# Moving GpSimd's sums for M and the dot products of layer 1 within a planned four-layer graph kernel

## Chip, cores and metric

The kernel runs on one core of a Trainium2 chip. The metric is the device time of one execution in microseconds. Before the change the median of three runs is 2234.3 us (2232.62 to 2236.04).

## What is computed

The input is 128 graphs of 128 nodes with 512 features, in float32, and one adjacency matrix of 128 by 128. Four layers follow one another, each a residual with a layer norm. Cut to what matters:

```python
y  = einsum('nm,bmd->bnd', adj, x);  x = norm(x + y @ W + bias)                # layer 0
q, k, v = x @ Wq.T, x @ Wk.T, x @ Wv.T                                         # layer 1
rel = adj.T * (q @ k.T);  rel = rel / norm_of_rows(rel);  x = norm(x + rel @ v)
h = x @ W2;  e = leaky(h @ a1 + (h @ a2).T) * adj                              # layer 2
x = norm(x + elu(softmax(e) @ h + beta * h))
x = norm(x + max(relu(A[:, :, None] + (C - A)[..., None])))                    # layer 3, A = adj x
```

In layer 1 the product of Wq and Wk is formed once, as M, so that q k' becomes (x M) x'. In layer 2 the scores h a1 and h a2 become dot products of the rows of x with two vectors W2 a1 and W2 a2 ("the dots"). They are taken of x before its layer norm and put right afterwards with the mean and the reciprocal deviation.

## The kernel before

The graphs are taken in 32 groups of four. Every group goes through the four layers, and the groups overlap like the stages of a pipeline: a group starts 28 slots after the one before it, and in one stretch of 28 slots (about 67 us) TensorE works on layer 0 of one group, layer 1 of the same and of the next, and layers 2 and 3 of older ones.

The order of the work is written by hand. `TABLE` gives each piece of a group's work a place in slots; `times(g)` adds 28 slots per group; `emit` collects (place, function) pairs; at the end the pieces are sorted by place and called (line 783). Each engine then runs its instructions in that order, since the engine wrappers keep the program's order. So the places decide only what comes before what on each of the engines; the waits between engines decide when.

The four large products (by W for y, by M, by Wv for v, by W2 for z) use a scheme with seven block products where a plain one needs eight. `left_factors` makes the four sums or differences of blocks on GpSimd (tile `s_x` for the products by M and Wv, `s_y`, `s_z` for the others); `product` issues seven steps on TensorE in the order 1, 2, 6, 5, 7, 3, 4. Steps 1, 2 and 4 read blocks of the transposed input itself (`xT`), steps 6 and 3 need the second and the fourth of GpSimd's sums, step 5 the first and step 7 the third. A finished region of PSUM is taken to SBUF by a copy on ScalarE or an addition on VectorE. Steps 1, 6, 7 and 4 share one PSUM region, so step 4 cannot start until VectorE's addition of step 7 (`tT<-r_m,tT`) has read it.

The pieces around the change, with the names that the profile shows:

- `x_sums` (left_factors, line 594): four GpSimd additions of 128x512 elements, `s_x<-xT`, `s_x<-s_x,xT`, `s_x<-xT`, `s_x<-xT,s_x`.
- `bias` (line 428): four GpSimd additions `x<-x,bias_sb` for the next group, each after TensorE's `p_y` of that graph has read x. After them come the four sums `s_y`.
- `residual` (line 545): VectorE, `x<-p_o,rn,x`, then `st` and `mv` (statistics).
- `dots` (line 559): VectorE, two `scr<-x,wa` per graph, eight per group, both operands in SBUF, each with an accumulator.
- `norm1` (line 379): VectorE's `ve`, then GpSimd's power `rstd`.
- `scale` (line 574): VectorE's `d<-mv,wa_sum,d` twice and `d<-d,rstd`. Layer 2's `p_s` on TensorE reads `d`.
- `elu` (line 716): VectorE's `x<-c,x` and `x<-m,x`, of an older group, again with both operands in SBUF.

Of the kernel before, what the change touches and what calls it, by code (L numbers as in the profile page):

```python
# [29 lines left out]
def kernel(  # L30
# [196 lines left out]
    def row(at, step, n=G):  # L227
        return [at + i * step for i in range(n)]


    TABLE = dict(
        load=[-20], y=row(0.5, 1), bias=row(1.3, 1), y_sums=row(5.2, 0.5), y_w=row(7, 1, 7),
        stats0=row(14.4, 0.4), norm0=[16.2], apply0=row(16.8, 0.33),
        turn=row(21.4, 1), turn_blocks=row(18.4, 0.6),
        move=row(20.5, 0.1), x_sums=row(25.3, 0.5), m=row(28, 1, 7), scores=row(36.5, 1),
        masked=[39.95], squares=[40.4], turn_rel=[40.3],
        move_rel=row(41.2, 0.1), inverse=[42.5], v=row(42, 1, 7), attend=row(50.6, 1),
        residual=row(51.0, 1), dots=row(54.2, 1.1), norm1=[55.2], scale=[58.8],
        apply1=row(65.4, 0.33),
        spread=[61.6], leaky=[62.0], weighted=[63.4], greatest=[64.3], exps=[64.4],  # L240
        divide=[65.8], turn_att=[68.6], with_beta=[69.0], gather=row(71.5, 1),
# [15 lines left out]
            scale=[5.6], apply1=row(24.3, 0.8), spread=[6.9], leaky=[7.4], weighted=[9.0],  # L257
# [8 lines left out]
            m=[0.0, 1.73, 3.46, 5.2, 7.4, 9.1, 10.8], scores=row(12.7, 0.9), masked=[16.4],  # L266
            squares=[17.2], turn_rel=[17.1], move_rel=row(18.0, 0.1), inverse=[20.0], v=[16.7, 18.4, 21.0, 22.7, 25.3, 27.9, 30.5],
            attend=row(33.2, 0.86), residual=row(34.1, 1.65), norm1=[40.65], dots=row(40.7, 1.53),
            scale=[47.0], apply1=row(47.5, 0.8), spread=[48.9], leaky=[49.4], weighted=[51.0],
# [544 lines left out]
```

## Time and profile before

The profile is one execution of 2234.4 us.

| engine | busy us | share | instructions |
|---|---|---|---|
| TensorE matmul (PE) | 2182.9 | 98% | 11073 |
| TensorE weight load (PEld) | 1842.1 | 82% | 11073 |
| VectorE (DVE) | 1794.9 | 80% | 3534 |
| ScalarE (ACT) | 980.0 | 44% | 1936 |
| GpSimd (POOL) | 983.1 | 44% | 743 |

A line of the timeline gives the start and the duration in us, the engine, the operation and the tiles as out<-in; a bracket gives the idle time of the engine before it and what ended it. A line of the costliest groups gives the count, the busy time, the mean duration of one and the idle time before. All calculations share one helper line (L26), so instructions are told apart by their tiles.

The work of a group repeats almost to 10 ns, so times below are often given relative to T, the start of the fourth `p_o` of a group (of its last graph's attention product). For the groups counted from 0, T is 299.45 for group 3, 366.27 for group 4 and 1042.01 for group 14.

### The profile page before, as it was taken

The page shows a single profiled execution, that of the slowest core. Times are in us where ns is not written, and L with a number is a line of the kernel's source. Part 1 is how long each engine was busy: PE and PEld are TensorE (multiplying, and loading weights), DVE is VectorE, ACT ScalarE, POOL GpSimd, SP SyncE. Part 2 cuts the span into 40 slices and gives each one's busy share as a digit, 9 for nine tenths or more (in the row PEclk, how much of TensorE's full clock was granted, in tenths as well). Part 3 has the DMA queues.
Part 4 walks back from the last instruction along what each step waited for, and adds up shares of the span by engine and source line. Part 5 has one row for each costly group of instructions (what it writes and reads, how often), then busy time and mean ns, then how long its engine had stood idle before and what let it go on. Part 6 is the DMA issues. An engine that isn't in the chain of part 4 may idle for free.

```text
span 2234.4 us, 31661 instructions
## 1 busy us (share of the span) xinstructions
PE 2182.9 (98%) x11073; PEld 1842.1 (82%) x11073; DVE 1794.9 (80%) x3534; ACT 980.0 (44%) x1936; POOL 983.1 (44%) x743
## 2 busy tenths in 40 slices
PE   7999999999999999999999999999999999999996
PEld 5888888888888888888888888888888888888873
DVE  4668888778878788888788888788888788887788
ACT  2224444444444454444444444444344444444535
POOL 3435454435455344544344554344553354443322
PEclk9999999999999999999999999999999999999998
DMA  4010222211222211222201222202222112221101
GB/s 166 25 32 19 60 57 62 62 28 40 60 59 62 62 19 48 59 60 62 59 19 52 58 61 62 52 22 55 57 62 63 41 28 59 58 62 43 21 28 57
DMA packets 333294, 115.15 MB, mean 52 GB/s; under 512 B 297424, under 2 KB 297552, under 8 KB 333136
## 3 DMA queue, kind: packets, MB, share of 16 engines
q1 hardware_dynamic: 331936, 110.77, 19.6%
q10 hardware_dynamic: 1200, 2.36, 0.3%
q8 instruction: 89, 1.46, 0.3%
q14 instruction: 69, 0.57, 0.1%
HBM read 39.65 MB, written 33.55 MB: 33 GB/s over the span
## 4 chain that ended last, share of the span: by engine, by line
PE 75%; DVE 20%; issue 3%; POOL 1%; ACT 1%; DMA 0%; DVEq 0%; ACTq 0%; POOLq 0%
PE r_v L26 17%; PE r_y L26 15%; PE r_z L26 14%; PE r_m L26 8%; DVE scr L26 6%; DVE x L26 6%; PE p_z L26 5%; PE p_o L26 5%; PE p_a L26 5%; PE p_rel L26 4%; DVE st L26 2%; PE p_y L26 2%; DVE tT L26 1%; DVE d L26 1%; PE p_m L26 1%
## 5 line engine op out<-in xcount | busy, mean ns | idle before, releaser
L26 ACT ACTIVATE x<-x,nmean,rstd 128x512 f32<-128x512 f32 x512 | 385.8, 808 | 187.5 <-DVE nmean L26 187.4
L26 DVE BATCH_NORM_STATS2 st<-x 128x6 f32<-128x512 f32 x512 | 352.1, 688 | 56.7 <-ACT x L26 47.9
L26 DVE SCALAR_TENSOR_TENSOR scr<-x,wa 128x512 f32<-128x512 f32 x256 | 286.2, 1169 | 0.0
L26 POOL TENSOR_TENSOR rstd<-ve,mhalf 128x4 f32<-128x4 f32 (+1 forms) x134 | 145.2, 1083 | 286.9 <-DVE ve L26 280.7
L26 POOL TENSOR_TENSOR x<-x,bias_sb 128x512 f32<-128x512 f32 x128 | 193.2, 1519 | 76.9 <-PE p_y L26 76.4
L26 POOL TENSOR_TENSOR s_x<-xT 128x512 f32<-128x512 f32 x64 | 95.8, 1497 | 256.5 <-DMA xT<-xB 237.6
L26 ACT ACTIVATE x<-x,top 128x512 f32<-128x512 f32 x128 | 92.4, 722 | 229.1 <-DVE top L26 228.8
L26 DVE TENSOR_TENSOR x<-r_y,x 128x512 f32<-128x512 f32 x224 | 151.4, 676 | 27.1 <-PE r_y L26 27.0
L26 ACT COPY c<-r_z 128x512 f32<-128x512 f32 x124 | 71.8, 579 | 221.5 <-PE r_z L26 221.5
L26 ACT COPY yT<-p_y 128x512 f32<-128x512 f32 x128 | 75.1, 587 | 206.5 <-PE p_y L26 206.5
L26 PEld LDWEIGHTS p_y<-adjT,x 128*128 128x128 f32 x1024 | 135.8, 195 | 13.1 <-ACT adjT L26 5.2
L26 DVE SCALAR_TENSOR_TENSOR x<-p_o,rn,x 128x512 f32<-128x512 f32 x128 | 95.9, 749 | 59.9 <-PE p_o L26 56.0
L26 PE MATMUL p_y<-adjT,x 128*128 128x128 f32 x1024 | 136.7, 278 | 6.4 <-ACT adjT L26 4.9
L26 PEld LDWEIGHTS p_z<-eT,x 128*128 128x128 f32 x1024 | 133.9, 192 | 8.4 <-DVE x L26 1.2
L26 DVE SCALAR_TENSOR_TENSOR x<-m,x 128x512 f32<-128x512 f32 x128 | 129.7, 1013 | 13.6 <-DVE x L26 0.9
L26 PEld LDWEIGHTS p_rel<-xT,tT 128*128 128x128 f32 x1024 | 134.1, 191 | 7.4 <-DVE tT L26 0.8
L26 POOL TENSOR_TENSOR s_z<-zT 128x512 f32<-128x512 f32 x31 | 39.3, 1267 | 224.0 <-ACT zT L26 224.0
L26 PE MATMUL p_rel<-xT,tT 128*128 128x128 f32 x1024 | 134.9, 275 | 0.6 <-DVE tT L26 0.6
L26 PE MATMUL p_z<-eT,x 128*128 128x128 f32 x1024 | 134.8, 275 | 0.4 <-DVE x L26 0.4
L26 PE MATMUL p_a<-x,adjT 128*128 128x512 f32 x256 | 131.2, 597 | 3.6 <-ACT x L26 1.9
L26 ACT COPY tT<-r_m 128x512 f32<-128x512 f32 x128 | 75.7, 591 | 132.9 <-PE r_m L26 132.9
L26 PE MATMUL p_o<-v,relT 128*128 128x512 f32 x256 | 130.3, 593 | 0.0
(119 smaller groups left out, 5008.6 us busy)
## 6 DMA issues: line engine op xcount, KB each, us to landing
out_dram<-x SPq DMA_DIRECT2D x128, 256.0 KB, 2.5
x<-in_x_dram SPq DMA_DIRECT2D x31, 1024.0 KB, 5.8
xT<-xB SPq DMA_DIRECT2D x480, 64.0 KB, 2.3
relT<-relB SPq DMA_DIRECT2D x512, 16.0 KB, 1.8
w_sb<-in_L_gnn_weight_dram ACTq DMA_DIRECT2D x1, 1024.0 KB, 5.9
x<-in_x_dram SPq DMA_DIRECT2D x4, 256.0 KB, 7.9
wq_sb<-in_L_gnn_Wq_dram SPq DMA_DIRECT2D x1, 1024.0 KB, 12.1
wk_sb<-in_L_gnn_Wk_dram SPq DMA_DIRECT2D x1, 1024.0 KB, 14.9
```

Source lines behind the costliest of these rows:

```text
L26: return lambda *args, **kw: self.tc.keep_in_program_order(op(*args, **kw))
```

## The change

Only places in the table change:

```diff
-        load=[-20], y=row(0.5, 1), bias=row(1.3, 1), y_sums=row(5.2, 0.5), y_w=row(7, 1, 7),
+        load=[-20], y=row(0.5, 1), bias=row(1.6, 1), y_sums=row(5.2, 0.5), y_w=row(7, 1, 7),
...
-        move=row(20.5, 0.1), x_sums=row(25.3, 0.5), m=row(28, 1, 7), scores=row(36.5, 1),
+        move=row(20.5, 0.1), x_sums=[27.95, 28.6, 30.0, 31.0], m=row(28, 1, 7), scores=row(36.5, 1),
...
-        residual=row(51.0, 1), dots=row(54.2, 1.1), norm1=[55.2], scale=[58.8],
+        residual=row(51.0, 1), dots=[51.7, 53.8, 54.9, 55.6], norm1=[54.6], scale=[57.2],
```

No instruction is added or taken away, and in the built program the order on TensorE, ScalarE and SyncE stays as it is. On the other two it becomes, for a group in the middle:

- GpSimd before: the four `s_x`, `rstd` of norm1, the four biases, the four `s_y`. After: `rstd`, `s_x` 1, `s_x` 2, bias 1, `s_x` 3, bias 2, `s_x` 4, bias 3, bias 4, the four `s_y`.
- VectorE before: the four residuals with their statistics (a `c<-r_z,c` addition among them), two dots, `c<-r_z,c`, `ve`, six dots, `tT<-r_m,tT`, `d` three times. After: residual 1, two dots, residuals 2 and 3, `c<-r_z,c`, two dots, residual 4, `ve`, `c<-r_z,c`, four dots, `d` three times, `tT<-r_m,tT`.

The aim is to have the dots run while GpSimd is not using SBUF, and to have GpSimd's sums for M made when the product by M begins, not as soon as the transposed input has landed.

## Prediction

> **What bounds it now.** I read the busy times first, then the waits of TensorE, then the timeline of several groups. The page's busy times:
>
> ```profile
> span 2234.4 us, 31661 instructions
> PE 2182.9 (98%) x11073; PEld 1842.1 (82%) x11073; DVE 1794.9 (80%) x3534; ACT 980.0 (44%) x1936; POOL 983.1 (44%) x743
> ```
>
> TensorE has work nearly always, so the change can only give or take its small stalls. From the timeline, the fourth `p_o` of group 1 starts at 162.96 and that of group 30 at 2124.63: 29 groups in 1961.67 us, a mean of 67.64. The shortest distance is 66.81 (group 2 to 3). So the stalls that a group could lose are worth 0.83 us, 24 us over the run. TensorE's waits name who makes them:
>
> ```profile
> PE r_m L26 <- DVE tT L26: 6.8, 5, 1.7
> PE r_y L26 <- DVE x L26: 4.4, 17, 0.4
> ```
>
> Both are VectorE being late, not GpSimd. VectorE is late from the dots on: they start at T+2.67 and VectorE is never idle again until about T+16.8 in the best groups. Why the dots are long is seen in the groups and in the timeline of group 3 (T=299.45):
>
> ```profile
> L26 DVE SCALAR_TENSOR_TENSOR scr<-x,wa 128x512 f32<-128x512 f32 x256 | 286.2, 1169 | 0.0
> ```
>
> ```profile
> 301.53 1.27 POOL L26 TENSOR_TENSOR s_x<-s_x,xT 128x512 f32<-128x512 f32 x1
> 302.13 1.23 DVE L26 SCALAR_TENSOR_TENSOR scr<-x,wa 128x512 f32<-128x512 f32 x1
> 302.76 1.73 POOL L26 TENSOR_TENSOR s_x<-xT 128x512 f32<-128x512 f32 x1
> 303.29 1.75 DVE L26 SCALAR_TENSOR_TENSOR scr<-x,wa 128x512 f32<-128x512 f32 x1
> 304.44 1.72 POOL L26 TENSOR_TENSOR s_x<-xT,s_x 128x512 f32<-128x512 f32 x1
> ...
> 306.71 0.68 DVE L26 SCALAR_TENSOR_TENSOR scr<-x,wa 128x512 f32<-128x512 f32 x1
> 307.32 0.68 DVE L26 SCALAR_TENSOR_TENSOR scr<-x,wa 128x512 f32<-128x512 f32 x1
> ```
>
> A dot takes 0.68 alone and 1.75 against a GpSimd addition, and that addition takes 1.72 in place of 1.27. The two take turns: the dot ends about 0.55 after the GpSimd addition that it waited for (302.80 to 303.36), and a GpSimd addition that waited ends 1.13 after the dot (303.36 to 304.49).
>
> **What the Trainium skill says.** "SBUF — State Buffer", section "Who interferes with whom", says that a VectorE instruction with two SBUF inputs contends with a GpSimd instruction that reads SBUF; the section "SBUF: two separate sides" says that the pair of ports is an exclusive lock, kept for the whole instruction by the one that starts first. The trace agrees: 0.68 against 1.75. Where a dot or an elu instruction and a GpSimd addition start within 0.25 us of each other in this trace, the earlier recorded start wins, down to a lead of 10 to 20 ns. Residuals, `tT`, `c` and the statistics (0.75, 0.67, 0.68 and 0.69) have at most one SBUF input tensor, and are never stretched.
>
> One more reading decides the case: the three small `d` instructions. In group 3 they take 0.79 and 0.17, because GpSimd then waits for TensorE's `p_y`. In group 1 (T=162.96) GpSimd has its biases queued without a break:
>
> ```profile
> 173.93 5.64 POOL L26 TENSOR_TENSOR x<-x,bias_sb 128x512 f32<-128x512 f32 x4
> 176.51 1.85 DVE L26 SCALAR_TENSOR_TENSOR d<-mv,wa_sum,d 128x4 f32<-128x4 f32 x2
> 178.46 1.13 DVE L26 TENSOR_TENSOR d<-d,rstd 128x8 f32<-128x8 f32 x1
> ```
>
> Then each of the three lets one whole GpSimd addition pass. A backlog on GpSimd taxes every VectorE instruction with two SBUF inputs by about 1.1 us, however short it is.
>
> **The change part by part.** It removes no work. The first four dots come into the gaps between `p_o` products and are uncontended: GpSimd's `rstd` of norm3 has ended by T-6.97 and nothing follows until norm1. Four dots at 0.61 from start to start fill what was mostly idle (0.89 before each of residuals 2 and 3 in group 3). Against that, `s_x` no longer starts at landing (T+0.6 to T+2.3 in groups 2 to 30) but after norm1's `rstd`, and `rstd`, four sums, four biases and then four `s_y` stand in one queue from there. Worked out for a middle group, in us after T, with the durations above:
>
> - `c` starts at 0.27 as before, dots at 0.87 and 1.48, residual 4 at 2.09, its statistics at 2.88 and 3.61, `ve` at 3.83 (0.22 after the aggregate, as in norm3 before) to 4.00, `rstd` to 5.09 (0.08 and 1.01), so `s_x` 1 starts at 5.07. VectorE's `c` follows `ve` at 3.91, dots at 4.51 and 5.12.
> - `s_x` 1 leads the second of these dots by 0.05 and gets the ports. Now they alternate: `s_x` 1 ends 6.34, dot 6.88, `s_x` 2 8.02, dot 8.56, bias 1 9.70, last dot 10.24, `s_x` 3 11.38, `d` 11.40, bias 2 12.61, `d` 12.63, `s_x` 4 13.84, `d` 13.86.
> - First `tT` 13.79 to 14.46, then elu: bias 3 ends 15.07, `x<-c` 15.6, bias 4 16.75, `x<-m` 17.3, statistics, second `tT` at 18.16.
> - `s_y` 1 ends 18.43; `s_y` 2 (18.51) leads the next `x<-c` (18.76) and ends 19.78; `x<-c` 20.33, `s_y` 3 21.46, `x<-m` 22.0, statistics, third `tT` at 22.86.
>
> TensorE needs `s_x` 2 at T+9.55 (1051.56 less 1042.01), `s_x` 3 at 14.79, `s_x` 4 at 16.52: all are ready, so the later sums cost TensorE nothing in a middle group. The later `bias` places only order GpSimd's queue. What is queued behind `rstd` is all of GpSimd's work, and VectorE's dots, `d` and elu meet it.
>
> What the third `tT` is worth is read from before. Its start and the distance to the next T: 21.11 and 66.82 (group 3), 22.43 and 67.75 (group 4), 22.68 and 68.01 (group 26), 23.97 and 69.29 (group 9). That is 66.82 plus whatever the third `tT` is past 21.5. So 22.86 gives 68.18: 0.54 more than the mean of 67.64, times 29 groups +15.7 us.
>
> The ends: in group 0 (T=99.06) no `p_y` lies in front and `s_x` 2 is needed at T+6.1; with residual 4 pushed to about T+4.9 by the four dots, `s_x` 2 ends near T+10.8, a stall of 4.8, for which the stalls of 2.24 at `p_s` and some 0.7 behind it go: about +1.9. In group 30 `d` comes about 1.0 earlier and 1.14 at `p_s` mostly goes: -0.8. Sum: 2234.3 + 15.7 + 1.9 - 0.8 = 2251.
>
> The unknown here is who wins two close races. `s_x` 1 against the second dot of graph 3 is a lead of 0.05 us, bounded by the losing orders in the rivals below. The second `d` lost in both groups of before with a queued bias (groups 0 and 1), so I take it as lost.
>
> **Rivals.** First, the dot wins the race for 5.1, or GpSimd starts `s_x` 1 a little later because of its eight landing waits. Then two dots are done one addition earlier: by the same steps the last dot ends at 9.2, `d` at 12.8, the second `tT` at 17.07, the third at 21.7, and a group takes 67.05: 29 times -0.59 is -17, 2218 with the ends. For it speaks that 0.05 is little; against it that the lead comes from well repeated durations. Second, the second `d` slips in before bias 2: the third `tT` comes at 21.5 and the group at 66.85, 2213; both together reach the floor of 66.81, 2211. Third, GpSimd is later still (the waits served only after `rstd`, or `s_x` 2 with its own wait), so that TensorE stalls at T+9.55: each 0.5 us is 14 us, some 2260; the 1.5 us of room speaks against it. Fourth, part of the groups goes each way: about 2234.
>
> **Numbers.** The alternating queue with all three `d` taxed: 0.57, with the third rival 0.02 of 2260 more. First rival 0.20, second 0.12, the mixture 0.09. The range reaches from the floor to a little above the sum: 2211 to 2257. Chances: faster 0.32, same 0.09, slower 0.59.
>
> **What would show it.** Right: the dots' mean falls from 1.17 to about 1.08 us, with five of eight at 0.68 and three at 1.75; GpSimd runs without a break from `rstd` to the last `s_y`; the `d` pair takes about 2.4 (two GpSimd additions) and `d<-d,rstd` about 1.1; the second `tT` starts near T+18.2, the third near T+22.9, each group takes 68.2, and TensorE's waits for `tT` and x grow. Wrong: third `tT` near 21.5 and groups of 66.8 to 67.1 (a race won by VectorE), or TensorE waiting for `s_x` in middle groups.

## The result and the profile after

The changed kernel takes 2255.98 us (2255.16 to 2257.07), against 2235.17 (2232.62 to 2237.45) for the kernel before in the same session: a ratio of 1.0094 with a 95% interval of 1.0076 to 1.0111. It is slower by 20.8 us; the forecast was 2251.

The page's busy times of the kernel after, which answer to those shown of before:

```profile
span 2254.1 us, 31660 instructions
PE 2198.8 (98%) x11073; PEld 1846.6 (82%) x11073; DVE 1849.9 (82%) x3534; ACT 980.0 (43%) x1936; POOL 964.4 (43%) x743
```

VectorE is busy 55 us longer with the same 3534 instructions, and GpSimd 19 us shorter. The groups of instructions show that it wasn't the dots that got longer. First two groups of before:

```profile
L26 DVE SCALAR_TENSOR_TENSOR x<-m,x 128x512 f32<-128x512 f32 x128 | 129.7, 1013 | 13.6 <-DVE x L26 0.9
L26 DVE SCALAR_TENSOR_TENSOR d<-mv,wa_sum,d 128x4 f32<-128x4 f32 x64 | 26.4, 450 | 0.0
```

Then three of after:

```profile
L26 DVE SCALAR_TENSOR_TENSOR scr<-x,wa 128x512 f32<-128x512 f32 x256 | 261.8, 1068 | 0.0
...
L26 DVE SCALAR_TENSOR_TENSOR x<-m,x 128x512 f32<-128x512 f32 x128 | 140.0, 1094 | 13.6 <-DVE x L26 0.9
...
L26 DVE SCALAR_TENSOR_TENSOR d<-mv,wa_sum,d 128x4 f32<-128x4 f32 x64 | 74.3, 1200 | 0.0
```

The mean dot fell from 1169 to 1068 ns, as intended. The mean `x<-m,x` rose from 1013 to 1094 ns: the elu meets more of GpSimd. The largest growth is in the smallest instructions: the pair `d<-mv,wa_sum,d` went from 26.4 to 74.3 us in all, and `d<-d,rstd` from 8.5 to 34.2. The waits of TensorE in after (us in total, times, longest):

```profile
PE r_y L26 <- DVE x L26: 11.9, 32, 0.9
PE r_m L26 <- POOL s_x L26: 6.8, 2, 5.1
```

The waits for VectorE's x grew from 4.4 us to 11.9; those for VectorE's `tT` (6.8 in before) fell to 0.4. The 5.1 us for `s_x` is a single stall, in group 0.

The middle groups are alike: from T=167.68 (group 1) to 2145.34 (group 30) the mean distance is 68.20 us, against 67.64 before. The timeline of group 14 in after (T=1054.04), VectorE and GpSimd with one line of TensorE, cut to what counts (the short reads of the accumulator between the dots are left out); the columns are start, duration, engine, operation and tiles:

```profile
1057.86 0.17 DVE L26 TENSOR_SCALAR ve<-mv 128x4 f32<-128x4 f32 x1
...
1058.11 1.01 POOL L26 TENSOR_TENSOR rstd<-ve,mhalf 128x4 f32<-128x4 f32 x1 [11.06 <-DVE ve L26]
1058.54 0.68 DVE L26 SCALAR_TENSOR_TENSOR scr<-x,wa 128x512 f32<-128x512 f32 x1
1059.09 1.26 POOL L26 TENSOR_TENSOR s_x<-xT 128x512 f32<-128x512 f32 x1
1059.15 1.75 DVE L26 SCALAR_TENSOR_TENSOR scr<-x,wa 128x512 f32<-128x512 f32 x1
1060.43 1.60 POOL L26 TENSOR_TENSOR s_x<-s_x,xT 128x512 f32<-128x512 f32 x1
...
1064.19 2.44 DVE L26 SCALAR_TENSOR_TENSOR d<-mv,wa_sum,d 128x4 f32<-128x4 f32 x2
1065.35 1.26 POOL L26 TENSOR_TENSOR x<-x,bias_sb 128x512 f32<-128x512 f32 x1
1066.57 1.27 POOL L26 TENSOR_TENSOR s_x<-xT,s_x 128x512 f32<-128x512 f32 x1
1066.74 1.13 DVE L26 TENSOR_TENSOR d<-d,rstd 128x8 f32<-128x8 f32 x1
...
1072.18 0.67 DVE L26 TENSOR_TENSOR tT<-r_m,tT 128x512 f32<-128x512 f32 x1
1072.90 1.99 PE L26 MATMUL r_m<-xT,t_m 128*128 128x256 f32 x8
...
1076.87 0.66 DVE L26 TENSOR_TENSOR tT<-r_m,tT 128x512 f32<-128x512 f32 x1
```

`s_x` 1 starts 0.06 before the dot at 1059.15, and the dot takes 1.75 in place of 0.68. From there the two engines alternate, through the dots and all three `d`, into the elu. TensorE's step 4 (1072.90) waits for the second `tT`, and the third `tT` comes at T+22.83.

### The profile page after: what moved, and what is told of

Read it like the earlier page. It is cut to its first block, busy times and chain, and to the rows that moved or that the text cites. A ratio compares the mean times of both kernels' runs of the same rounds, so it can differ in the third digit from the quotient of the medians.

```text
span 2254.1 us, 31660 instructions
## 1 busy us (share of the span) xinstructions
PE 2198.8 (98%) x11073; PEld 1846.6 (82%) x11073; DVE 1849.9 (82%) x3534; ACT 980.0 (43%) x1936; POOL 964.4 (43%) x743
## 4 chain that ended last, share of the span: by engine, by line
PE 61%; DVE 33%; issue 3%; POOL 1%; ACT 1%; DMA 0%; DVEq 0%; ACTq 0%; POOLq 0%
PE r_v L26 17%; PE r_y L26 13%; PE r_z L26 12%; DVE x L26 10%; DVE scr L26 9%; PE p_z L26 5%; PE p_a L26 5%; DVE st L26 4%; PE p_o L26 4%; PE p_rel L26 4%; DVE d L26 3%; DVE tT L26 3%; DVE c L26 2%; PE r_m L26 1%; DVE e L26 1%
## 5 line engine op out<-in xcount | busy, mean ns | idle before, releaser
L26 POOL TENSOR_TENSOR rstd<-ve,mhalf 128x4 f32<-128x4 f32 (+1 forms) x134 | 133.0, 993 | 632.6 <-DVE ve L26 617.6
L26 DVE SCALAR_TENSOR_TENSOR scr<-x,wa 128x512 f32<-128x512 f32 x256 | 261.8, 1068 | 0.0
L26 POOL TENSOR_TENSOR x<-x,bias_sb 128x512 f32<-128x512 f32 x128 | 188.5, 1475 | 25.2 <-PE p_y L26 25.0
L26 DVE TENSOR_TENSOR x<-r_y,x 128x512 f32<-128x512 f32 x224 | 151.5, 677 | 25.5 <-PE r_y L26 25.3
L26 DVE SCALAR_TENSOR_TENSOR x<-m,x 128x512 f32<-128x512 f32 x128 | 140.0, 1094 | 13.6 <-DVE x L26 0.9
L26 DVE TENSOR_TENSOR v<-r_v,v 128x512 f32<-128x512 f32 x96 | 65.8, 685 | 80.3 <-PE r_v L26 77.6
L26 PE MATMUL r_m<-s_x,t_m 128*128 128x256 f32 x512 | 123.2, 384 | 6.9 <-POOL s_x L26 6.8
```

Of the source, the lines that this page charges most:

```text
L26: return lambda *args, **kw: self.tc.keep_in_program_order(op(*args, **kw))
```

## Experiments

What differs is the order of two queues, so each experiment moves one thing in one queue, or takes one suspected cost out. Times are medians; "group" is the mean distance from T to T of the 29 middle groups.

**The dots alone.** GpSimd's order goes back to that of before; the dots, `ve` and `d` stay moved. (The sums have a step of 0.4 slots and not 0.5, which keeps the fourth ahead of `rstd`, whose place is now earlier.)

```diff
-        ... bias=row(1.6, 1), ...
-        ... x_sums=[27.95, 28.6, 30.0, 31.0], ...
+        ... bias=row(1.3, 1), ...
+        ... x_sums=row(25.3, 0.4), ...
```

> The sums for M and the biases go back, so that GpSimd's order is that of the kernel before; the dots, ve and d keep their new places. Theory (ports in turn): GpSimd then has its sums done by about T+7 and has to wait for p_y in front of biases 2, 3 and 4, so the three d instructions and the first elu fall into its gaps; the second tT starts at 16.8, a group takes 66.8 to 67.0, and the run about 2208 to 2215 us (ratio to before 0.988 to 0.991). Rival (the new order on VectorE is itself what costs, whatever GpSimd does): 2250 or more.

Measured: 2210.73 us (2210.43 to 2211.22), 0.9887 [0.987, 0.9903] of before. The group is 66.81, the shortest that any kernel here showed. The timeline of its group 14 (T=1030.59):

```profile
1032.85 1.27 POOL L26 TENSOR_TENSOR s_x<-xT 128x512 f32<-128x512 f32 x1 [9.24 <-DMA xT<-xB]
...
1040.08 2.45 DVE L26 SCALAR_TENSOR_TENSOR d<-mv,wa_sum,d 128x4 f32<-128x4 f32 x2
...
1042.63 0.17 DVE L26 TENSOR_TENSOR d<-d,rstd 128x8 f32<-128x8 f32 x1
...
1043.01 1.28 POOL L26 TENSOR_TENSOR x<-x,bias_sb 128x512 f32<-128x512 f32 x1 [0.51 <-PE p_y L26]
...
1047.38 0.69 DVE L26 TENSOR_TENSOR tT<-r_m,tT 128x512 f32<-128x512 f32 x1 [0.80 <-PE r_m L26]
1047.99 0.70 DVE L26 SCALAR_TENSOR_TENSOR x<-c,x 128x512 f32<-128x512 f32 x1
```

The sums start when `xT` has landed, T+2.26, and by T+12 GpSimd has caught up: it waits for TensorE's `p_y`, so `d<-d,rstd` takes 0.17 and not 1.13. Not everything fell into gaps as expected: in this group the `d` pair still takes 2.45. At the second `tT` it is VectorE that waits 0.80 for TensorE. That is the slack of which the changed kernel has none. So the half of the change that moves the dots is worth -25.3 us by itself, and this version is faster than both kernels. The rival, that VectorE's new order is what costs, falls.

**The sums alone.** The kernel before with only GpSimd's new places:

```diff
-        ... bias=row(1.3, 1), ...
-        ... x_sums=row(25.3, 0.5), ...
+        ... bias=row(1.6, 1), ...
+        ... x_sums=[27.95, 28.6, 30.0, 31.0], ...
```

> Only the sums for M and the biases move; dots, ve and d stay where they were before. Theory (ports in turn): ve is at T+4.5, the first sum starts at about 5.7, six of the eight dots stand against GpSimd's queue and the last ends at 12.6; the second tT comes at 19.4, the third at 24.1, a group takes 69.4, and the run about 2290 us (1.024), so that moving the dots gave back more than half of what moving the sums cost. Rival (the late sums cost the 21 us of the change and the dots brought nothing): about 2256.

Measured: 2265.28 us (2261.78 to 2269.71), 1.0132 [1.0114, 1.015] of before; the group is 68.57. The direction is as expected, the size is not: +29 us where +55 was expected. Three steps of the expected path came otherwise in every middle group. Its group 3 (T=301.46):

```profile
306.18 1.38 POOL L26 TENSOR_TENSOR rstd<-ve,mhalf 128x4 f32<-128x4 f32 x1 [11.70 <-DVE ve L26]
...
306.62 0.69 DVE L26 SCALAR_TENSOR_TENSOR scr<-x,wa 128x512 f32<-128x512 f32 x1
...
307.23 0.69 DVE L26 SCALAR_TENSOR_TENSOR scr<-x,wa 128x512 f32<-128x512 f32 x1
...
307.53 1.51 POOL L26 TENSOR_TENSOR s_x<-xT 128x512 f32<-128x512 f32 x1
...
316.49 0.68 DVE L26 SCALAR_TENSOR_TENSOR x<-c,x 128x512 f32<-128x512 f32 x1
316.50 3.48 POOL L26 TENSOR_TENSOR x<-x,bias_sb 128x512 f32<-128x512 f32 x2
```

`rstd` starts beside a dot and takes 1.38, not 1.01; `s_x` 1 comes at T+6.07 and not at the expected 5.7; the dots end at T+11.5 and not at 12.6. But this does not decide the size. What decides it is a later race, at T+15.03, between the first `x<-c` of the elu and the third bias. In group 3 `x<-c` goes first and takes 0.68. In group 5 (T=437.90) it loses and takes 1.83:

```profile
452.93 2.96 POOL L26 TENSOR_TENSOR x<-x,bias_sb 128x512 f32<-128x512 f32 x2
452.93 1.83 DVE L26 SCALAR_TENSOR_TENSOR x<-c,x 128x512 f32<-128x512 f32 x1
```

`x<-c` wins in 21 of the 29 middle groups: there the third `tT` starts at about T+22.82, as in the changed kernel, and the group takes 68.2. It loses in 8: there the second `tT` comes at 19.4, the third at 24.1 and the group takes 69.4 or more, all as expected. An estimate from these figures: had it lost in the other 21 too, 21 times 1.2 us more would give about 2290, the size expected. So this kernel is a mixture of two outcomes, and that most groups went the cheaper way was not foreseen. The rival (about 2256) falls as well. The moves don't add up: moving the sums costs 29 us when the dots are at their old places and 45 us when they have been moved (2210.73 to 2255.98).

**`ve` behind `c`.** Is it that `s_x` 1 starts just ahead of the dot? VectorE's `ve` and the following `c<-r_z,c` change places, so that GpSimd starts a little later.

```diff
-        ... norm1=[54.6], ...
+        ... norm1=[54.8], ...
```

> The changed kernel with norm1 at 54.8 in place of 54.6: on VectorE ve and the addition c<-r_z,c behind it trade places, nothing else. GpSimd's rstd and so its first sum start about 0.45 us later. Theory (who is first at the ports): one more dot is done before the first sum, and from there VectorE is one GpSimd addition ahead: d ends at 12.6, the second tT comes at 16.9, the third at 21.5, a group takes 66.8 and the run about 2217 us. Rival (GpSimd's queue starts too late, and each delay of it is passed on): 2256 or slower, up to 2269 (29 groups by 0.45).

Measured: 2226.68 us (2224.3 to 2227.36), 0.9956 [0.9941, 0.9971] of before. One swap of a 0.17 us instruction takes 29 us off the changed kernel; the group is 67.08. Its group 3 (T=302.54):

```profile
307.06 1.38 POOL L26 TENSOR_TENSOR rstd<-ve,mhalf 128x4 f32<-128x4 f32 x1 [11.50 <-DVE ve L26]
...
308.11 0.68 DVE L26 SCALAR_TENSOR_TENSOR scr<-x,wa 128x512 f32<-128x512 f32 x1
...
308.41 1.51 POOL L26 TENSOR_TENSOR s_x<-xT 128x512 f32<-128x512 f32 x1
...
319.84 1.26 POOL L26 TENSOR_TENSOR s_y<-yT 128x512 f32<-128x512 f32 x1
319.94 1.72 DVE L26 SCALAR_TENSOR_TENSOR x<-c,x 128x512 f32<-128x512 f32 x1
```

Seven dots of eight now run free and only one is taxed. `s_x` 1 starts at T+5.87 and not at 5.05, so this moves GpSimd by 0.8 us and is not a test of 0.05 us alone. The rival, that a later GpSimd only passes its delay on (2256 or slower), falls. What was missing against the expected 2217 has its place too: `s_y` 1 leads the second `x<-c` by 0.10 us, which takes 1.72 in place of the 0.70 of the dots-alone kernel. The third `tT` comes at T+21.65 and not 20.63, and each group costs 0.24 to 0.27 more than the floor: 7 to 8 us.

**Without `d`.** How much do three instructions cost that need some 0.96 us when nothing hinders them (0.79 and 0.17 in group 3 of before)? The changed kernel with the three `d` instructions left out: layer 2 then gets the dots without their correction by mean and deviation.

```diff
-                dve.scalar_tensor_tensor(s["d"][:, i, :], s["mv"][:, :, 0], ...)
...
-            dve.tensor_tensor(s["d"], s["d"], s["r", 0]..., ALU.mult)
```

> The changed kernel without the three small d instructions per group: the dots go to layer 2 without the mean's part and the reciprocal deviation. Alone these three take 0.8 to 1.0 us. Theory (each lets one GpSimd addition pass): they cost VectorE about 3.4 us, without them it reaches the first elu before its operand is there, the second tT starts at 16.8, a group takes 66.8 and the run about 2217 us. Rival (they cost what they take alone, about 0.9 us): the third tT at about 21.9, a group 67.2 to 67.3, the run about 2230.

Measured: 2218.49 us (2217.75 to 2219.18), 0.9921 [0.9907, 0.9936] of before; the group is 66.91, that is 1.28 less than in after. So the three are on the path with more than the time that they need alone, and the rival, that they cost only this (about 2230 us), falls. On VectorE itself they cost 3.6: the first `tT` comes at T+10.15, not 13.75, the sum of what they take in after (2.44 and 1.13). In its group 3 (T=300.99) VectorE waits for others where it was late in after:

```profile
311.14 0.68 DVE L26 TENSOR_TENSOR tT<-r_m,tT 128x512 f32<-128x512 f32 x1
...
314.99 0.80 DVE L26 SCALAR_TENSOR_TENSOR x<-m,x 128x512 f32<-128x512 f32 x1 [2.11 <-ACT m L26]
...
317.78 0.69 DVE L26 TENSOR_TENSOR tT<-r_m,tT 128x512 f32<-128x512 f32 x1 [1.04 <-PE r_m L26]
```

**GpSimd later still.** If a later start of `s_x` 1 is what helps, then useless work on GpSimd should help. The changed kernel with one more power of a 128x4 tile behind `rstd` in every group:

```diff
+        def idle_power():
+            q = small.tile([P, G], FP, tag="idle", name=f"idle_{g}")
+            pool.tensor_tensor(q, s["r", 0], mhalf, ALU.pow)
...
+        emit(t["norm1"][0], idle_power)
```

> The changed kernel with one more GpSimd instruction per group, right behind rstd of norm1: the same power of a 128x4 tile into a tile that nobody reads, about 1.0 us. VectorE's order is untouched, so this only makes GpSimd's sums later. Theory (who is first at the ports): the first sum starts at T+6.1, two more dots are done alone before it, VectorE is one addition ahead from there, the sum that TensorE needs at T+9.55 ends at about 9.2, the third tT is at 21.0 to 21.7 and a group takes 66.8 to 67.1 in place of 68.2: 2219 to 2226 us with one more us at the start, so useless work makes the kernel some 30 us faster. Rival (GpSimd's queue is too late, a delay of it is passed on): 2256 if it is hidden, 2285 if it is passed on in full.

Measured: 2233.42 us (2232.37 to 2233.73), 0.9986 [0.998, 0.9993] of before. The added work makes the changed kernel 22.6 us faster, so the rival, that a delay of GpSimd is hidden or passed on (2256 to 2285), falls. From its group 3 (T=302.55):

```profile
307.70 1.50 POOL L26 TENSOR_TENSOR idle<-rstd,mhalf 128x4 f32<-128x4 f32 x1
308.27 0.69 DVE L26 SCALAR_TENSOR_TENSOR scr<-x,wa 128x512 f32<-128x512 f32 x1
...
309.18 1.51 POOL L26 TENSOR_TENSOR s_x<-xT 128x512 f32<-128x512 f32 x1
```

```profile
323.41 0.66 DVE L26 TENSOR_TENSOR tT<-r_m,tT 128x512 f32<-128x512 f32 x1
...
327.86 0.69 DVE L26 TENSOR_REDUCE nm<-e 128x4 f32<-128x512 f32 x1 [1.80 <-POOL e L26]
```

All eight dots are free (their mean is 687 ns on this kernel's page) and the third `tT` comes at T+20.86, near that of the dots-alone kernel. Yet the group is 67.31, not 66.81: the delay comes out at the other end of GpSimd's queue, where VectorE now waits 1.80 for GpSimd's `e`, behind the last `s_y`. The size expected (2219 to 2226) left that end out. Against the dots-alone kernel, TensorE in group 14 is 0.10 late from T+9.87, right behind `s_x` 2 (which ends at T+9.50), and 0.38 more at `r_y<-t,yT`, T+35.48. So the wait for `e` can make up the larger part of the 0.5 at most; it was not tried by itself.

**Group 0 alone.** The result lay 5 us above the forecast, and group 0 seemed the place. The changed kernel with the sums of group 1, which are made in the stretch after T of group 0, at their old places:

```diff
-    FIRST = {0: dict(turn=row(20.4, 0.3)), 1: dict(y=row(-9.5, 0.3), bias=row(-9.2, 0.3))}
+    FIRST = {0: dict(turn=row(20.4, 0.3)), 1: dict(x_sums=row(25.3, 0.5), y=row(-9.5, 0.3), bias=row(-9.2, 0.3))}
```

> The changed kernel with the sums for M of group 1 alone at their old places (25.3, 25.8, 26.3, 26.8), which TensorE waits for in group 0's stretch. Theory: the stall of 5.1 us and the low clock behind it go, T of group 1 comes 5.6 us earlier as in the run with all sums back (63.5 in place of 69.1 after group 0's), the other groups keep 68.2: about 2250.4 us (0.9975 of the changed kernel). Rival (the late start is made up later, or group 0's stall only moves to p_s): 2254 to 2256.

Measured: 2252.67 us (2249.69 to 2252.98), 1.0067 [1.0054, 1.008] of before. T of group 1 is 163.28 and not 167.68; the middle groups stay at 68.20. The stretch from T of group 0 to T of group 1 is 5.0 us shorter (64.14 for 69.10). Only 3.3 us of this reach the end. T of group 0 itself is 0.6 later (99.14 for 98.58); it lies between 98.44 and 99.15 in the eight profiles and follows nothing that was moved. And near the end of the run TensorE has a clock of 0.50 for some 3 us in this profile and not in that of after, which costs 1.0. Two of the five runs took 2249.7 and 2249.9, below the expected 2250.4, and three 2252.7 to 2253.0. The rival (2254 to 2256) falls: group 0's stretch made some 5 us of the loss. What these consist of is seen in windows of the start, first of after, then of this kernel. The columns are the window, its length, the busy time and count of PE, PEld, DVE, ACT and POOL, the granted clock, the DMA share and GB/s:

```profile
105.00:110.00 5.00, 0.08 (x1) 0.08 (x1) 4.97 (x12) 0.46 (x1) 4.58 (x4) 0.87 0.58 210
110.00:113.20 3.20, 3.20 (x8) 2.55 (x9) 2.83 (x3) 0.00 (x0) 3.20 (x3) 0.50 0.02 5
113.20:116.00 2.80, 2.80 (x13) 2.62 (x12) 0.00 (x0) 0.55 (x2) 2.07 (x3) 0.58 0.00 0
```

```profile
105.00:110.00 5.00, 5.00 (x32) 4.59 (x31) 4.90 (x13) 1.66 (x3) 3.60 (x3) 1.00 0.61 213
110.00:113.20 3.20, 3.20 (x19) 2.89 (x19) 3.10 (x3) 1.08 (x2) 3.20 (x3) 1.00 0.00 0
```

In after, TensorE stands still from 105 to 110, and then has a clock of 0.50 and 0.58 for 6 us: 8 matmuls in 3.20 us, where the other kernel, without the stall, does 19 at 1.00.

## Why the prediction was right

**What bounds the kernel** held: TensorE stays at 98%, and what is lost are its small stalls behind VectorE.

**The chain of a middle group** held in every step to about 0.05 us. In group 14 of after, against the working:

| step, us after T | predicted | measured |
|---|---|---|
| `ve` starts | 3.83 | 3.82 |
| `s_x` 1 starts | 5.07 | 5.05 |
| second dot of graph 3 starts | 5.12 | 5.11 |
| `d` pair takes | about 2.4 | 2.44 |
| `d<-d,rstd` takes | about 1.1 | 1.13 |
| second `tT` starts | 18.16 | 18.14 |
| third `tT` starts | 22.86 | 22.83 |
| group | 68.18 | 68.20 |

29 groups cost +16.0 us for +15.7 predicted. The race for 0.05 us, on which most of the chances lay, went the same way in all 29 groups, so the mixture did not happen. The durations repeat well enough for a lead of 0.05 us to decide, as the working assumed. They don't for 0.02: the close race of the sums-alone kernel went both ways. One sign did not come: the waits for `tT` were to grow and fell from 6.8 us to 0.4. The 6.8 belonged to five groups of before that took 69.3 to 69.7; the change replaced groups of 66.8 to 69.7 by groups of 68.2 throughout.

**The tax on short instructions** was argued from group 1 of before and is now shown: leaving out `d` gave back 37.5 us. The Trainium skill ("SBUF — State Buffer", "SBUF: two separate sides") has a lock that is kept for the whole instruction by the one that starts first; this is how 0.96 us of work come to cost 1.28 on the path of every group, and these runs agree with it for the additions (`d<-d,rstd` 1.13 in after, 0.17 where GpSimd waits for `p_y`). For GpSimd's power they don't: `rstd` runs from 1058.11 to 1059.12, and the dot that starts inside it, at 1058.54, is not held and takes 0.68.

**From the third `tT` to the group**: the rule read from before (66.82 and whatever is past 21.5) gave 68.18 for 68.20 in after, and the other kernels fit it roughly (24.09 with 69.42 in part of the sums-alone kernel, 21.65 with 67.08, 21.49 with 66.91, 20.63 with 66.81); it fails in the kernel with the useless power (20.86 with 67.31), where a second wait comes behind `tT`. How the lateness is passed on is seen at TensorE, in group 14 of after:

```profile
1078.77 0.68 DVE L26 TENSOR_TENSOR x<-r_y,x 128x512 f32<-128x512 f32 x1
...
1079.60 1.97 PE L26 MATMUL r_y<-t,s_y 128*128 128x256 f32 x8 [0.36 <-DVE x L26]
...
1089.33 0.69 DVE L26 TENSOR_TENSOR x<-r_y,x 128x512 f32<-128x512 f32 x1
...
1090.07 1.59 PEld L26 LDWEIGHTS r_y<-t,yT 128*128 128x128 f32 x8 [0.28 <-DVE x L26]
```

Each time, a step of TensorE needs a PSUM region that VectorE has to read first, as step 4 does behind the second `tT`. Against the dots-alone kernel, group 14 of after is later by 0.18 at step 4 (T+18.86, T+18.68), by 0.80 at `r_y<-t,s_y` (25.56, 24.76), by 1.25 at this `r_y<-t,yT` (36.03, 34.78) and by 1.35 at the `r_v` that follows (37.86, 36.51). From there to the next T nothing is added (68.16, 66.81). So a group's loss is made by a few short handovers from a late VectorE; the wait list names only parts of it, since the first matmuls behind each wait are longer too (1.97 to 1.99 for eight, 1.89 otherwise).

**The mis-sized term** is group 0, predicted at +1.9 and measured at +4.7. The stall for `s_x` 2 was about right: 5.1 us for 4.8. Left out was the granted clock behind this stall. After it, eight matmuls of 128x256 took 3.78 us, then `p_y` 1.91 and the next eight 2.06, for 1.89, 1.05 and 1.89 at the full clock: 2.9 us lost. In before, the stall of 2.1 at `p_s` was also followed by slow matmuls (3.44 and 0.83, for 1.99 and 0.60 in the kernel without either stall), 1.7 us that fall away, where the working had 0.7. So 5.1 + 2.9 - 2.1 - 1.7 is 4.2. Another 1.0 is lost at one place further on, ahead of the first `r_y<-t,s_y` of this stretch, where TensorE waits 0.85 for VectorE's x; before did not wait there. Together they make the 5.2 by which T1 - T0 grew (63.90 to 69.10). That T of group 0 comes 0.5 earlier belongs to no term, and leaves 4.7. The end behind group 30 was -1.0 for -0.8. Together the terms miss 2.9 of the 5.0 us. The other 2 are a matter of the base: a run's time lies some 2.2 above its profiled span (2236.61 and 2234.4 in before, 2256.3 and 2254.1 in after), and the terms, read from spans, were added to a median of 2234.3, which is 2.3 below the time of the profiled execution.

The range reached up to 2257, 1 us above what was measured. That the path was right is shown; that a group 0 mis-sized by 2.8 us and the low base still fitted was luck.

**The rivals** were possible orders of the same two queues. Making the dot win its race, by the swap of `ve`, gives 2226.68, on the way to the 2218 that the first rival worked out, with a different path to it: `rstd` is also lengthened, more dots go free, and the start stays dear. A TensorE stall at T+9.55 in every group did not occur in the changed kernel.

## What to carry to other kernels

Before moving work into a stretch where an engine "is quiet", list what queues behind the point where that engine starts again: here the halves of one change gave -25.3 us and +29 us alone, because the second half rebuilt the queue that the first avoided. Where two engines take turns for a whole instruction, count turns and not microseconds, and place short two-input instructions where the other engine waits for something else. Where a race is closer than 0.02 us, as in the sums-alone kernel, work out both outcomes: it can be a mixture. And price a stall of 2 us or more with the slow clock that followed each of them here, not only with its length.

## What was not expected of the hardware

- A GpSimd power of only 128x4 also waits for a dot in progress: `rstd` took 1.01 alone, 1.38 beside a dot, and the useless power 1.50. It was there to see in before (1.39 in group 3), but the workings took 1.01. The other way round it does not hold: a dot that starts during the power takes 0.68.
- An instruction with one SBUF input can be taxed too: `ve`, a `TENSOR_SCALAR` of 128x4, took 0.17 in after, where GpSimd was waiting, 0.62 in group 3 of before and 1.08 in group 14 of the dots-alone kernel, in both of these ending 0.02 behind the GpSimd addition in progress.
- Which of two starts is the earlier by the record does not tell the winner within 0.02 us: in the sums-alone kernel `x<-c` led the bias by 18 ns in five groups that it lost, and by 1 to 19 ns in the 21 that it won.
- Useless work of 1.0 us per group on an engine that is busy 43% made the kernel 22.6 us faster, since it shifted who starts first.
- The slow clock behind a stall does not follow from the stall's length alone. From 95 us on, all seven stalls of TensorE of 2 us or more in the eight profiles were followed by a clock of 0.50 for some us (1.7 us lost behind 2.1, 2.9 behind 5.1). Behind shorter ones it came or not: the same stall of 1.72 us near the end of the run was followed by 0.50 in three of the eight profiles and by 1.00 in five.
- A few groups are some 0.3 us longer in several kernels; their cause stays open.
